# A fourteenth room in a shared arena, paid for with three smaller buffers, and tile 30's output moved from GpSimd to VectorE

## The chip, the cores and the metric

The kernel runs on one core of one Trainium2 chip. The metric is device time in microseconds of one execution, the median over several runs. Engine names in profile rows: PE is the TensorE matmul unit and PEld its weight load, DVE is VectorE, ACT is ScalarE, POOL is GpSimd, and SP is SyncE, which here only issues DMAs. A "q" behind an engine's name means its sequencer, which waits, branches and issues, while the engine itself does not work.

## The reference, cut to what matters

The input x has 8 batches of 512 rows and 512 columns; there are 16 heads of 32 columns. A single token per batch is projected too and added to every query and every key.

```python
Q, K, V = heads(x @ Wq.T + bq), heads(x @ Wk.T + bk), heads(x @ Wv.T + bv)
cQ = Q + heads(cond @ Wq.T + bq)
cK = K + heads(cond @ Wk.T + bk)
attn = softmax(cQ @ cK.T / sqrt(32))        # per batch and head, 512 x 512
out = x + merge_heads(attn @ V)
```

All data are 32-bit floats. The softmax's arguments are shifted by each row's own maximum.

## The kernel before, in words

**Tiles.** The work is cut into T = 32 tiles: tile t is batch t // 4 and head group t % 4, four heads of 32 columns, which fill 128 partitions. A tile needs projections of q, k and v (shared by pairs of tiles), scores with their row maxima (`row_max`, line 617 on PE, lines 584 and 626 on DVE), exponentials on ACT, the product with V on PE (`times_v`, line 745), and at last a division, the bias and the residual x (`send`, lines 811 to 814).

**Two kinds of tiles.** Odd tiles from 1 to 27 are "blocked". `denominators` (line 664) writes their exponentials with queries on the partitions, and the matmul with V needs keys there. So `exchange` sends them through 16 DMAs per half tile, each of which moves 32 partitions of one room to another quarter of the tile `blocks`, and then DVE transposes `blocks` in place in squares of 32 (`turn_blocks`, line 637, eight pieces per tile). All other tiles compute the scores a second time with keys on the partitions; `exponentials` (lines 717 to 734) does this in four steps kc = 0 to 3.

**The arena.** `arena` is a tile of 13 rooms of 4 KB per partition. A blocked tile always uses rooms 0 to 7 (`rows_kept`: rooms 0 to 3 for its first half, 4 to 7 for its second). The other tiles take two rooms per step kc from a counter, which is set to room 8 when the next tile is blocked. Even tile t therefore uses rooms 8, 9 (kc 0), 10, 11 (kc 1), 12 and 0 (kc 2), 1 and 2 (kc 3). The blocked tile t + 1 is being made in the same stretch of time: its first half lies in rooms 0 to 3 and is copied out by `exchange(t + 1, 0)`. Room 0 may be overwritten in step kc 2 only after the four DMAs that read it have landed.

**The order of the work.** For PE, ACT, DVE and POOL the order is that of the source, written out by hand: each tile's turn in the main loop (t = 1 to 28) is four items, "V" (product with V of tile t - 1), "q", "k" and "v" (projections), and each item carries one step of exponentials where t is even, one quarter of the next tile's scores, and small work. DMAs on SP are placed by the framework's planner, which follows the order of the source as far as buffers are free in its own estimate; SP then works through its list in order. DMAs that POOL issues (in `exchange` the sources on partitions 96 to 127, `BY_POOL = (3,)`) stand in POOL's own order.

**Products of blocks.** Projections use seven products of half blocks instead of eight (`MADE_OF`). Four combinations of blocks of x are kept in `xc` (four slots of 2 KB per partition) and made anew for each batch by `combine_x`: lines 385 and 386 for the first half, 388 and 389 for the second, on POOL except for one on DVE. Product 5 uses combination 0, which is x block (0,1) minus x block (0,0). No product uses block (0,1) of x itself.

**Residuals and output.** `load_residual` (line 194) loads x once more for a pair of tiles into one of two buffers with the tag "xr"; `add_bias` (line 207, POOL) adds the bias for v. `send` copies a tile's transposed result to a buffer "res" (two of them) and finishes it on POOL, lines 813 and 814.

**The start.** Tile 0 has its own written order ahead of the loop: four steps of exponentials, each beside one half of a v projection. **The end.** Tiles 29 to 31 have one too. Tile 30's output is finished at lines 1272 to 1275 (DVE transposes, then POOL multiplies by the reciprocal sums and adds the residual), and three of its four stores are issued at line 1280 while tile 31 is finished on DVE and PE (lines 1291 to 1314); the fourth is issued last of all. Line 1352 is the end of the program, where each engine runs a DRAIN and all meet at a barrier.

Of the kernel before, what the change touches and what calls it, by code (L numbers as in the profile page):

```python
# [9 lines left out]
F32 = mybir.dt.float32  # L10
BF16 = mybir.dt.bfloat16
AF = mybir.ActivationFunctionType
ALU = mybir.AluOpType
# [4 lines left out]
def kernel(  # L18
# [38 lines left out]
    nc = tc.nc  # L57
    P = 128
# [4 lines left out]
    HG = P // HD  # L63
# [4 lines left out]
    T = B * G  # L68
    HS = S // 2

    ROOMS = 13
    BY_POOL = (3,)
    WARM = (48, 8, 8)
    BLOCKED = list(range(1, T - 4, 2))
# [1 line left out]
    const = ctx.enter_context(tc.tile_pool(name="const", bufs=1))  # L76
# [5 lines left out]
    op = ctx.enter_context(tc.tile_pool(name="op", bufs=2))  # L82
# [37 lines left out]
    def banks(i, n=1):  # L120

        row = row_of[0] or [at_end[j] for j in TURNS[turn[0]]]
        j = row[i]
        if n == 1:
            return psum[:, j, :]
        k = row[i + 1]
        return psum[:, j : k + 1 : k - j, :]
# [24 lines left out]
    BL = 32  # L152
    NB = S // BL

    def spread(a, d, n=1):

        return a.rearrange("(f j) d -> j f d", j=BL)[:, :, d : d + n * BL]
# [14 lines left out]
    xr = {}  # L172
# [7 lines left out]
    def load_residual(t):  # L180

        b, g = divmod(t, G)
        if t == T - 1:

            xr[t] = xT[b][:, g, :]
        elif late:
            xr[t] = late_part(t % 2 * 10 + 2).rearrange("p (f e) -> p f e", e=BL)
            for h in range(HG):
                nc.sync.dma_start(xr[t][h * BL : (h + 1) * BL], spread(x[b], h * P + g * BL))
        else:  # L190
            two = op.tile([P, NB, 2, BL], F32, tag="xr", name=f"xr_{t}", bufs=2)
            twos[t // 2] = two
            for h in range(HG):
                nc.sync.dma_start(
                    two[h * BL : (h + 1) * BL].rearrange("p f c e -> p f (c e)"),
                    spread(x[b], h * P + g * BL, 2),
                )
            for i in range(2):
                xr[t + i] = two[:, :, i, :]
# [8 lines left out]

    arena = ep.tile([P, ROOMS, NP * S], F32, tag="arena", name="arena")
    place = [0]  # L210

    def room_for_e(t, kc, pr):
# [3 lines left out]
        i = place[0]  # L216
        place[0] = (i + 1) % ROOMS
        return arena[:, i, :].rearrange("p (i s) -> p i s", s=S)
# [102 lines left out]
    condT = early[:, 7, : NC * HD].rearrange("p (c e) -> p c e", e=HD)  # L321
    identb = const.tile([P, P], BF16, tag="identb", name="identb")
    nc.vector.tensor_copy(identb, ident)
    xc = const.tile([P, 4, 2, HS], F32, tag="xc", name="xc")
    vs = [const.tile([P, NS, D], F32, tag=f"v{i}", name=f"v{i}") for i in range(2)]


# [31 lines left out]
    xT = {}  # L359
# [18 lines left out]
    def combine_x(b, half, on=nc.vector):  # L378

        if b >= B:  # L380
            return
        blk = [[xT[b][:, i * 2 : i * 2 + 2, j * HS : (j + 1) * HS] for j in range(2)] for i in range(2)]
        to = [xc[:, i, :, :] for i in range(4)]
        if half == 0:
            on.tensor_tensor(to[2], blk[1][1], blk[0][1], ALU.subtract)
            on.tensor_tensor(to[1], to[2], blk[0][0], ALU.add)
        else:
            on.tensor_tensor(to[0], blk[0][1], blk[0][0], ALU.subtract)
            on.tensor_tensor(to[3], blk[1][0], to[1], ALU.subtract)
# [51 lines left out]

    def block_of_x(b, i, kc, at):
        f = MADE_OF[i - 1][1]
        if isinstance(f, int):
            return xc[:, f, kc, at]
        off = HS * (f == "22")
        return xT[b][:, kc + 2 * (f != "11"), at.start + off : at.stop + off]

    def product(n, b, u, i, pt, kcs=(0, 1)):

        for kc in kcs:
            w = block_of_w(n, i, u, kc)
            if n == "v":
                still, moving = block_of_x(b, i, kc, slice(u * P, (u + 1) * P)), w
            else:
                still, moving = w, block_of_x(b, i, kc, slice(0, HS))
            for j in range(HG):
                r = slice(j * HD, (j + 1) * HD)
                nc.tensor.matmul(  # L459
                    pt[r], still[:, r], moving, start=(kc == kcs[0]), stop=(kc == kcs[-1])  # L460
                )
# [83 lines left out]
    def other_products(n, b, u, dens, small, at):  # L545

        dens()
        one_, two_ = banks(at[0]), banks(at[1])
        product(n, b, u, 4, one_[:, :HS])
        product(n, b, u, 5, one_[:, HS:])  # L550
        small()
        product(n, b, u, 2, two_[:, :HS], (1,))
        product(n, b, u, 3, two_[:, HS:])
        c1, c12, c2, c22 = parts_of(n, b, u)
        nc.vector.tensor_tensor(c12, one_[:, HS:], c12, ALU.add)
        nc.vector.tensor_tensor(c2, halves(one_), twice(c22), ALU.add)
        plus(n, b, u, 0, c1, halves(two_), c1)
        if n != "v":
            for g in range(2):
                qkT[n, b * G + u * 2 + g] = pair_of(b * G + u * 2, n)[:, g, :]  # L560
# [78 lines left out]
    def exchange(t, half):  # L639

        if t not in blocked:
            blocked[t] = room(f"blocks_{t}")
        for g in (0, 2, 1, 3):
            for a in range(HG):
                queue = nc.gpsimd if a in BY_POOL else nc.sync
                of = arena[a * BL : (a + 1) * BL, half * HG + g, :]
                to = blocked[t][g * BL : (g + 1) * BL, a, half * 2 : half * 2 + 2]
                queue.dma_start(to.rearrange("p c h s -> p (c h s)"), of)  # L648

    def denominators(t, qc, w=HG):  # L650

        if t >= T - 2:
            return
        for j in range(HG):
            if t in BLOCKED:
                to = rows_kept(t, qc // 2)[:, :, qc % 2, j, :].rearrange(
                    "p g (c e) -> p g c e", e=BL
                )
            else:
                to = banks(w + j)  # L660
            of = banks(w + j)
            if t in BLOCKED:
                of = of.rearrange("p (c g e) -> p g c e", g=HG, e=BL)
            nc.scalar.activation(  # L664
                to,
                of,
                AF.Exp,
                bias=nmax[t][:, qc, j, :],
                accum_out=sums[t][:, qc, j, :],
            )  # L670
# [137 lines left out]

    def send(t, y_, rec):

        y = op.tile([P, NB, BL], F32, tag="res", name=f"res_{t}", bufs=2)
        nc.vector.transpose(y.rearrange("p f e -> p (f e)"), y_)  # L812
        nc.gpsimd.tensor_tensor(y, y, rec.broadcast_to([P, NB, BL]), ALU.mult)  # L813
        nc.gpsimd.tensor_tensor(xr[t], y, xr[t], ALU.add)  # L814
        if t % 2 or t >= T - 4:
            to_store.append(t)
# [17 lines left out]
    def untranspose(o, pt):  # L834
        for qc in range(NS):
            nc.tensor.transpose(  # L836
                pt[:, qc * P : (qc + 1) * P], o[:, qc * P : (qc + 1) * P], ident
            )
# [136 lines left out]
    def late_part(i):  # L975
        return late[0][:, i, :]
# [36 lines left out]
        )  # L1013
    load_residual(0)
    add_bias(0)
    load_residual(2)

    exponentials(0, 0)
    row_max(1, 1)
# [20 lines left out]
    exponentials(0, 3)  # L1040
    row_max(2, 0)
    other_products("v", 0, 1, lambda: denominators(2, 0), nothing, (0, 2))

    def products(t, n, blocks, hold, dens, small):

# [35 lines left out]
    for t in range(1, T - 3):  # L1081
        b, r = divmod(t, G)
# [116 lines left out]
    t = T - 3  # L1199
# [22 lines left out]
    t = T - 2  # L1222
# [28 lines left out]
    t = T - 1  # L1251
# [17 lines left out]
    rec = op.tile([P, NB, 1], F32, tag="recs", name=f"recs_{t - 1}")  # L1269
    nc.vector.reciprocal(rec, den[:, :, 0:1])  # L1270
    y30 = late_part(13).rearrange("p (f e) -> p f e", e=BL)
    nc.vector.transpose(y30.rearrange("p f e -> p (f e)"), parts[t - 1])
    x30 = xr.pop(t - 1)
    nc.gpsimd.tensor_tensor(y30, y30, rec.broadcast_to([P, NB, BL]), ALU.mult)
    nc.gpsimd.tensor_tensor(y30, y30, x30, ALU.add)

    def store_30(queue, hs):
        b, g = divmod(t - 1, G)
        for h in hs:
            queue.dma_start(spread(out[b], h * P + g * BL), y30[h * BL : (h + 1) * BL])  # L1280

    store_30(nc.sync, (0, 1))
    exponentials(t, 3, (4, 2, 0, 1))
    times_v(t, 2, pv)
    pd = bank(7)
# [5 lines left out]
    nc.vector.tensor_tensor(part_x, pd, xr[t], ALU.mult)  # L1291
    den = late_part(11)
    nc.scalar.copy(den, pd)
    store_30(nc.scalar, (2,))
    oT = late[0][:, 0, :]
    y = late[0][:, 1, :].rearrange("p (c s) -> p c s", c=NS)
    rec = op.tile([P, NS, HG, 1], F32, tag="rec", name="rec")
    pi, po = bank(6), [bank(4), bank(2)]
    b, g = divmod(t, G)
    two = [slice(0, HS), slice(HS, S)]  # L1300
    for i in range(2):
        nc.vector.tensor_tensor(oT[:, two[i]], pv[:, two[i]], part_x[:, two[i]], ALU.add)  # L1302
        for qc in (i * 2, i * 2 + 1):
            nc.tensor.transpose(  # L1304
                po[i][:, qc * P : (qc + 1) * P], oT[:, qc * P : (qc + 1) * P], ident
            )
        if i == 0:
            untranspose(den, pi)
    nc.vector.reciprocal(  # L1309
        rec, pi.rearrange("p (c h e) -> p c h e", c=NS, h=HG)[:, :, :, 0:1]  # L1310
    )
# [45 lines left out]
```

## Time and profile before

| what | value |
|---|---|
| median of 3 runs | 681.99 us (680.9, 681.99, 684.14) |
| profiled execution | 682.65 us, of which the span from first to last instruction is 680.4 us |
| PE busy | 660.6 us, 97% |
| DVE busy | 578.9 us, 85% |
| ACT busy | 544.6 us, 80% |
| POOL busy | 340.7 us, 50% |
| mean granted TensorE clock | 0.994 |

The page's first part gives busy time per engine. The timeline lists instructions in order of time with their start, duration and count; the bracket at a row's end is the engine's idle time just ahead of it and what ended it. The view of a source line lists all instructions that bear its number with shortest, median and longest duration and the start of the first and the last.

### The profile page before, as it was taken

To read this page: it belongs to the slowest core of one execution; us is meant where nothing else is said; L and a number is where in the kernel's file an instruction comes from. 1 tells how busy PE (TensorE), PEld (TensorE's weight loads), DVE (VectorE), ACT (ScalarE), POOL (GpSimd) and SP (SyncE) were. 2 spreads that over 40 slices of the span, in tenths; PEclk is the share of its full clock that TensorE was granted. 3 is DMA by queue.
4 is the path that set the end of the run, shared out by engine and by line. 5 is a ranking of instruction groups with operands and counts; after the bars stand their busy time and mean duration, and the time that the engine had idled before them with its cause. 6 is when DMAs were issued, how large, how long until landed. Compare 5 with 4: busy or idle time off the path is not lost. (4 is left out here: it accounts for less than half of the span.)

```text
span 680.4 us, 22874 instructions
## 1 busy us (share of the span) xinstructions
PE 660.6 (97%) x9100; PEld 312.6 (46%) x9100; DVE 578.9 (85%) x821; ACT 544.6 (80%) x1397; POOL 340.7 (50%) x449
## 2 busy tenths in 40 slices
PE   7989999999999999999999999999999999999993
PEld 6444454544544444444544444454544544454421
DVE  5897988989899898979889897898989898897793
ACT  1568788988979898898889888788988989897771
POOL 5551563565446464466635664464644666352531
PEclk9999999999999999999999999999999999999997
DMA  9718439386574938658383865729376573822011
GB/s 203 129 29 206 126 68 224 69 200 152 128 190 85 223 79 209 142 133 208 71 223 70 211 139 134 188 67 237 80 201 151 132 178 66 220 47 56 16 18 32
DMA packets 140814, 90.85 MB, mean 134 GB/s; under 512 B 117436, under 2 KB 126308, under 8 KB 140708
## 3 DMA queue, kind: packets, MB, share of 16 engines
q1 hardware_dynamic: 132196, 73.78, 47.5%
q0 software_dynamic: 5568, 14.95, 8.7%
q8 instruction: 72, 1.18, 0.8%
q10 hardware_dynamic: 2944, 0.66, 0.5%
q14 instruction: 34, 0.28, 0.1%
HBM read 20.27 MB, written 8.39 MB: 42 GB/s over the span
## 5 line engine op out<-in xcount | busy, mean ns | idle before, releaser
L664 ACT ACTIVATE psum<-psum,nmax 128x512 f32<-128x512 f32 x256 | 169.0, 663 | 52.5 <-DVE nmax L584 40.1
L584 DVE TENSOR_REDUCE nmax<-psum 128x1 f32<-128x512 f32 x270 | 171.4, 680 | 46.0 <-PE psum L617 45.5
L734 ACT ACTIVATE arena<-psum 128x512 f32<-128x512 f32 x264 | 136.9, 602 | 33.8 <-PE psum L723 24.4
L617 PE MATMUL psum<-kT,qT 32*128 32x512 f32 x1024 | 157.5, 621 | 1.4 <-ACT psum L664 1.4
L664 ACT ACTIVATE arena<-psum,nmax 128x512 f32<-128x512 f32 x224 | 152.6, 697 | 5.3 <-issue 4.2
L626 DVE TENSOR_REDUCE nmax<-psum 128x2 f32<-128x1024 f32 x115 | 139.3, 1212 | 1.1 <-PE psum L617 1.1
L637 DVE STREAM_TRANSPOSE blocks<-blocks 128x1024 f32<-128x1024 f32 x112 | 132.2, 1218 | 0.3 <-DMA blocks<-arena 0.2
L648 POOL DMA_DIRECT2D blocks<-arena x112 | 56.1, 506 | 78.8 <-ACT arena L664 69.2
L813 POOL TENSOR_TENSOR res<-res,recs 128x512 f32<-128x512 f32 x30 | 31.5, 1049 | 120.9 <-DVE res L812 120.9
L617 PEld LDWEIGHTS psum<-kT,qT 32*128 32x128 f32 x1024 | 59.5, 182 | 64.9 <-issue 24.0
L745 PE MATMUL psum<-arena,v 128*32 128x512 f32 x576 | 69.4, 597 | 0.0
L723 PE MATMUL psum<-qT,kT 32*128 32x512 f32 x528 | 68.5, 589 | 0.0
L745 PE MATMUL psum<-blocks,v 128*32 128x256 f32 x896 | 52.1, 381 | 0.0
L459 PE MATMUL psum<-wc_v,xc 128*32 128x256 f32 x768 | 50.6, 381 | 1.4 <-ACT v L497 1.4
L664 ACT ACTIVATION_READ_ACCUMULATOR psum<-psum,nmax 128x1 f32 x256 | 51.9, 203 | 0.0
L664 ACT ACTIVATION_READ_ACCUMULATOR arena<-psum,nmax 128x1 f32 x224 | 47.8, 213 | 0.0
L459 PE MATMUL psum<-xc,wc_q 128*32 128x256 f32 x720 | 47.4, 381 | 0.0
L459 PE MATMUL psum<-xc,wc_k 128*32 128x256 f32 x720 | 47.4, 381 | 0.0
L812 DVE STREAM_TRANSPOSE res<-psum 128x512 f32<-128x512 f32 x28 | 20.1, 717 | 23.3 <-PE psum L745 23.3
L814 POOL TENSOR_TENSOR xr<-res,xr 128x512 f32<-128x512 f32 x30 | 38.5, 1282 | 2.4
L207 POOL TENSOR_TENSOR xr<-xr,wT_q 128x512 f32<-128x512 f32 x30 | 38.4, 1279 | 0.2
L745 PEld LDWEIGHTS psum<-blocks,v 128*32 128x32 f32 x896 | 26.4, 110 | 25.0 <-ACT arena L734 10.6
(184 smaller groups left out, 934.4 us busy)
## 6 DMA issues: line engine op xcount, KB each, us to landing
blocks<-arena SPq DMA_DIRECT2D x336, 128.0 KB, 3.8
blocks<-arena POOLq DMA_DIRECT2D x112, 128.0 KB, 3.9
xr<-in_x_dram SPq DMA_DIRECT2D x60, 128.0 KB, 2.6
x<-in_x_dram SPq DMA_DIRECT2D x56, 128.0 KB, 3.5
out_dram<-xr SPq DMA_DIRECT2D x56, 128.0 KB, 2.4
w_q<-in_L_cond_Wq_dram SPq DMA_DIRECT2D x4, 256.0 KB, 4.4
w_k<-in_L_cond_Wk_dram SPq DMA_DIRECT2D x4, 256.0 KB
w_v<-in_L_cond_Wv_dram SPq DMA_DIRECT2D x4, 256.0 KB, 8.3
```

Source lines behind the costliest of these rows:

```text
L207: nc.gpsimd.tensor_tensor(xr[t], xr[t], bias, ALU.add)
L459: nc.tensor.matmul(pt[r], still[:, r], moving, start=(kc == kcs[0]), stop=(kc == kcs[-1]))
L584: nc.vector.tensor_reduce(nmax[t][:, qc, j : j + 1, 0], pt, AX.X, ALU.max, negate=True)
L617: nc.tensor.matmul(pt, qkT["q", t][r, qc * P : (qc + 1) * P], qkT["k", t][r, :], start=True, stop=True,)
L626: nc.vector.tensor_reduce(nmax[t][:, qc, pr * 2 : pr * 2 + 2, 0], pt, AX.X, ALU.max, negate=True)
L637: nc.vector.transpose(e, e)
L648: queue.dma_start(to.rearrange("p c h s -> p (c h s)"), of)
L664: nc.scalar.activation(to, of, AF.Exp, bias=nmax[t][:, qc, j, :], accum_out=sums[t][:, qc, j, :],)
L723: nc.tensor.matmul(bank[j], qkT["k", t][r, kc * P : (kc + 1) * P], qkT["q", t][r, :], start=False, stop=True,)
L734: nc.scalar.activation(e[:, i, :], bank[pr * 2 + i], AF.Exp)
L745: nc.tensor.matmul(pt[j * HD : (j + 1) * HD, at], vs[b % 2][:, kc, (g * HG + j) * HD : (g * HG + j + 1) * HD], e, start=(kc == chunks[0]), ...
L814: nc.gpsimd.tensor_tensor(xr[t], y, xr[t], ALU.add)
```

## The change

- `ROOMS` goes from 13 to 14. An even tile then uses rooms 8 and 9, 10 and 11, 12 and 13, 0 and 1.
- The room is paid for by 4 KB per partition elsewhere: `res` has one buffer instead of two (2 KB), and `xc` three slots instead of four (2 KB). Combination 0 is made in place over block (0,1) of x for batches 1 to 7; for batch 0, whose x is still needed whole, it lies in one of the two "xr" buffers until tile pair 2 takes that buffer.
- `load_residual(2)` moves from ahead of tile 0's four steps to behind them, since its buffer is taken until then.
- `exchange` issues the groups in the order 0, 1, 2, 3 instead of 0, 2, 1, 3.
- Tile 30: the multiplication goes from POOL to DVE at the same place, and the addition goes to DVE behind tile 31's two additions at line 1302 and ahead of the reciprocal at line 1309. The three stores follow the addition.

```diff
-    ROOMS = 13
+    ROOMS = 14
...
-    xc = const.tile([P, 4, 2, HS], F32, tag="xc", name="xc")
+    xc = const.tile([P, 3, 2, HS], F32, tag="xc", name="xc")
+    x0c = op.tile([P, 2, 2, HS], F32, tag="xr", name="x0c", bufs=2)[:, 0]
+
+    def in_place(b):
+
+        return xT[b][:, 0:2, HS:] if b else x0c
...
-        to = [xc[:, i, :, :] for i in range(4)]
+        to = [in_place(b), *(xc[:, i, :, :] for i in range(3))]
...
         f = MADE_OF[i - 1][1]
+        if f == 0:
+            return in_place(b)[:, kc, at]
         if isinstance(f, int):
-            return xc[:, f, kc, at]
+            return xc[:, f - 1, kc, at]
...
-        for g in (0, 2, 1, 3):
+        for g in range(HG):
...
-        y = op.tile([P, NB, BL], F32, tag="res", name=f"res_{t}", bufs=2)
+        y = op.tile([P, NB, BL], F32, tag="res", name=f"res_{t}", bufs=1)
...
     add_bias(0)
-    load_residual(2)
...
     other_products("v", 0, 1, lambda: denominators(2, 0), nothing, (0, 2))
+    load_residual(2)
...
-    nc.gpsimd.tensor_tensor(y30, y30, rec.broadcast_to([P, NB, BL]), ALU.mult)
-    nc.gpsimd.tensor_tensor(y30, y30, x30, ALU.add)
+    nc.vector.tensor_tensor(y30, y30, rec.broadcast_to([P, NB, BL]), ALU.mult)
...
-    store_30(nc.sync, (0, 1))
...
-    store_30(nc.scalar, (2,))
...
         if i == 0:
             untranspose(den, pi)
+    nc.vector.tensor_tensor(y30, y30, x30, ALU.add)
+    store_30(nc.sync, (0, 1))
+    store_30(nc.scalar, (2,))
     nc.vector.reciprocal(
```

## The prediction

> **What bounds the kernel now.** I read the page first, then the table of waits, then the timeline at three places: the start, one turn of the loop, and the end.
>
> ```profile
> span 680.4 us, 22874 instructions
> PE 660.6 (97%) x9100; PEld 312.6 (46%) x9100; DVE 578.9 (85%) x821; ACT 544.6 (80%) x1397; POOL 340.7 (50%) x449
> ```
>
> PE is busy 97% of the span, and no row of the change takes a matmul away. So it can gain only where PE is kept waiting, and behind PE's last work. There are three such places.
>
> *Start.* ACT, PE and SP, timeline (start, duration, both in us):
>
> ```profile
> 59.33 1.09 ACT L734 ACTIVATE arena<-psum 128x512 f32<-128x512 f32 x2
> 62.83 1.09 ACT L734 ACTIVATE arena<-psum 128x512 f32<-128x512 f32 x2 [2.42 <-DMA blocks<-arena]
> ...
> 47.49 0.40 PE L720 MATMUL psum<-wT_v,onesb 3*128 3x512 bf16 x4
> 52.72 0.40 PE L720 MATMUL psum<-wT_v,onesb 3*128 3x512 bf16 x4
> 58.05 0.39 PE L720 MATMUL psum<-wT_v,onesb 3*128 3x512 bf16 x4
> 65.24 0.73 PE L720 MATMUL psum<-wT_v,onesb 3*128 3x512 bf16 x4
> 71.15 1.14 PE L617 MATMUL psum<-kT,qT 32*128 32x512 f32 x8
> ...
> 51.03 2.84 SPq L194 DMA_DIRECT2D xr<-in_x_dram  x4
> 55.56 2.39 SPq L167 DMA_DIRECT2D x<-in_x_dram  x4
> 58.26 17.96 SPq L648 DMA_DIRECT2D blocks<-arena  x24
> 85.42 1.33 SPq L694 DMA_TRANSPOSE wT_v<-split  x1
> ```
>
> In step kc 2 of tile 0 ACT writes room 12 at 59.33, then stands 2.42 us for the DMAs that read room 0, which SP began to issue at 58.26. PE pays: the steps begin at 47.49, 52.72 and 58.05, 5.23 and 5.33 apart. The next is 7.19 later, and the one behind it 5.91. Against 5.23 and 5.33 that is 1.96 + 0.58 = 2.5 us lost.
>
> *Loop.* ACT's first exponentials in the turns of tiles 2, 24 and 26, and step kc 2 and 3 of tile 4:
>
> ```profile
> 91.12 2.06 ACT L734 ACTIVATE arena<-psum 128x512 f32<-128x512 f32 x4
> 528.19 2.06 ACT L734 ACTIVATE arena<-psum 128x512 f32<-128x512 f32 x4
> 567.62 1.57 ACT L734 ACTIVATE arena<-psum 128x512 f32<-128x512 f32 x3
> ...
> 141.53 1.08 ACT L734 ACTIVATE arena<-psum 128x512 f32<-128x512 f32 x2
> 143.78 1.08 ACT L734 ACTIVATE arena<-psum 128x512 f32<-128x512 f32 x2 [1.17 <-issue]
> 147.42 1.59 ACT L734 ACTIVATE arena<-psum 128x512 f32<-128x512 f32 x3
> ```
>
> Two turns without a wait take 567.62 - 528.19 = 39.43 us. The twelve pairs of turns from 91.12 to 567.62 take 476.50, where 12 x 39.43 = 473.16: 3.34 us are lost in some of them. Tile 4 shows how: the first two of step kc 2 (room 12) run at 141.53, the next two (room 0) come 1.17 us late. The view names "issue" as the cause, but POOL's share of the copy tells it:
>
> ```profile
> 138.83 2.00 POOL L648 DMA_DIRECT2D blocks<-arena  x4
> DMA to landing us min/median/max: 2.3/3.8/6.5
> 501.69 2.12 SPq L648 DMA_DIRECT2D blocks<-arena  x2
> 509.18 1.23 DVE L637 STREAM_TRANSPOSE blocks<-blocks 128x1024 f32<-128x1024 f32 x1
> ```
>
> POOL issues the read of room 0's last quarter at 138.83. With 3.8 us to land, the median of these DMAs, it is done at 142.6, the moment at which ACT is ready (141.53 + 1.08). Each landing over the median stalls ACT, and PE behind it. It is a lottery drawn anew in each turn; the runs' spread from 680.9 to 684.14 is of the same size.
>
> *End.* The rows of line 1352, the end of the program, SP's wait there, and the last work of each engine:
>
> ```profile
> L1352 POOLq DRAIN x3: 46/102/11037, 668.6 to 680.1; - x3
> L1352 SPq DRAIN x3: 7/7/7, 674.8 to 679.9; - x3
> L1352 DVEq DRAIN x2: 19/340/661, 670.7 to 679.9; - x2
> SPq L1352 <- PEq L1352: 5.0, 1, 5.0
> 651.96 1.27 POOL L814 TENSOR_TENSOR xr<-res,xr 128x512 f32<-128x512 f32 x1
> 666.76 0.65 DVE L1272 STREAM_TRANSPOSE late<-parts 128x512 f32<-128x512 f32 x1
> 667.97 0.69 DVE L1291 TENSOR_TENSOR late<-psum,xT 128x512 f32<-128x512 f32 x1 [0.55 <-PE psum L755]
> 668.62 1.27 POOL L1275 TENSOR_TENSOR late<-late 128x512 f32<-128x512 f32 x1
> 668.80 0.76 DVE L1302 TENSOR_TENSOR late<-psum,late 128x256 f32<-128x256 f32 x2
> 669.92 0.85 SPq L1280 DMA_DIRECT2D out_dram<-late  x2
> 670.19 0.26 DVE L1309 RECIPROCAL rec<-psum 128x16 f32<-128x16 f32 x1 [0.63 <-PE psum L836]
> ```
>
> The longest of POOL's three drains takes 11.04 us. The first starts at 668.6, the last at 680.1, so only the first can be that long: it ends at 679.6. SP has seen all stores land and drains at 674.8, then waits 5.0 us at the barrier. So the span is ended by POOL's drain, not by the chain of waits through PE and DVE. Its end lies 9.73 us behind POOL's last operation, the addition of tile 30 (668.62 + 1.27 = 669.89).
>
> **The change part by part.**
>
> *Room 14, start.* Step kc 2 of tile 0 goes to rooms 12 and 13; nothing reads 13. The wait of 2.42 us goes. Room 0 is next wanted in step kc 3, which PE begins at 65.24 - 2.5 = 62.7 and whose exponentials follow 1.3 us later, as 59.33 follows 58.05: at 64.0. SP's three DMAs that read it are the first at 58.26, 17.96 / 24 = 0.75 us apart; the third goes out at 59.8 and, with a median landing (3.8 us), is done at 63.6. Room 1 follows by 0.5 to 1 us on both sides. That is tight, but no longer late. Bounds -2.5 (PE's count) to 0; I take -2.4, ACT's own row.
>
> *Room 14, loop.* Room 0 is wanted at step kc 3, 147.42 - 143.78 = 3.64 us later than now, room 1 1.0 us behind it. The plain order lets group 1 go out second, so both have some 4 us of margin where room 0 has none. All 3.34 us go; bounds -3.34 and 0.
>
> *Plain order of groups.* The same 32 DMAs. What waits for all four groups is DVE's first transpose: in the tightest tile SP has issued at 503.81 and DVE comes at 509.18, 5.4 us later, against landings of 3.8, at most 6.5. Cost 0; no row shows neighbouring groups in this order, so its upper end is the slower rival below, its lower end 0.
>
> *One "res".* DVE's copy must now wait until POOL has read the copy before.
>
> ```profile
> L813 POOL TENSOR_TENSOR res<-res,recs 128x512 f32<-128x512 f32 x30 | 31.5, 1049 | 120.9 <-DVE res L812 120.9
> ```
>
> POOL waits for DVE's copy (120.9 us over 30), not the other way round: the buffer is long free. 0.
>
> *Combination in place.* The same POOL operation, 1.28 us. A price would come if waits went by whole stretches of xT, for product 1's operand lies between the two pieces written:
>
> ```profile
> 157.15 1.07 PE L459 MATMUL psum<-xT,wT_q 128*32 128x256 f32 x16
> 159.38 1.29 POOL L388 TENSOR_TENSOR xc<-xT 128x512 f32<-128x512 f32 x1
> ...
> 106.89 8.41 SPq L648 DMA_DIRECT2D blocks<-arena  x12
> 111.54 1.23 DVE L637 STREAM_TRANSPOSE blocks<-blocks 128x1024 f32<-128x1024 f32 x1
> ```
>
> PE would then wait 160.67 - 157.15 = 3.5 us in seven batches, 24.6 us. But DVE's transpose at 111.54, whose pieces lie on both sides of what the second half's DMAs write, runs while those are still being issued (to 115.30). Waits go by exact elements: 0, upper end 24.6.
>
> *Residual 2.* Its four DMAs (2.84 us of SP) leave 51.03 and go behind the step in which PE last reads the buffer, 65.24 to 71.15. SP is not sooner free for the copies: x at 55.56 stands ahead of them. Behind them SP has nothing from 76.22 to 85.42, so 2.84 us fit. If the planner puts them ahead of the copy's second half, that lands 2.1 to 2.8 us later and can meet DVE's transposes: between 0 and +0.5; I take 0.
>
> *Tile 30 on VectorE.* POOL loses two operations, so its last one is the row at 651.96. DVE gains two. A like operation, 128x512 with both inputs in SBUF:
>
> ```profile
> 65.72 0.68 DVE L385 TENSOR_TENSOR xc<-xT 128x512 f32<-128x512 f32 x1
> ```
>
> The multiplication fits at 667.41, where DVE is idle 0.55 us until PE is done: 0.68 - 0.55 = 0.13 late for line 1291, which line 1302 hides (it waits for PE until 668.8). The addition starts at 669.56 and ends at 670.24; DVE was idle 0.63 there, the reciprocal comes 0.05 late. The stores go out at 670.3 instead of 669.92, ahead of tile 31's at 671.0. Cost +0.1, at most +0.7 (one whole operation). And the drain: if it follows POOL's last operation by 9.73 us, it ends near 653.23 + 9.73 = 663, and SP's drain at 674.84 opens the barrier: 679.62 - 674.84 = 4.78 less. Bounds -4.78 and 0; I take -4.7. For it: DVE's drain (670.7 + 0.66) ends when DVE is through with its own last work, so a drain looks at its engine; and no other row of the trace ends near 679.6.
>
> The Trainium skill ("VectorE: DVE Perf Modes", "The DRAIN you can't avoid") says that the drains of a program's start and end take about 12 ns on all five engines; SP's 7 ns agree, POOL's 11.04 us do not, and the row decides. "PSUM — Partial Sum Buffer" ("Engine vs sequencer instructions") says that a drain waits for its own engine to be idle, which is the reading taken.
>
> *Sum*, against the profiled execution: 682.65 - 2.4 - 3.34 - 4.7 + 0.1 = 672.3. That execution stands 0.66 over the median of the runs, by its draw of loop waits, which the change removes; so the sum needs no correction to that median. **Forecast 672.3 us**, 1.4% under 681.99. Half a per cent, 3.4 us, is about what a measurement of this kernel can tell from no change.
>
> **The rivals.**
>
> *The drain does not follow POOL's last operation* but something that stays where it is, such as the last stores. For it: only one drain of this kind is in the trace, so no row shows its dependence. Against: SP sees the last store 5 us earlier. Then 682.65 - 5.7 + 0.1 = 677.0.
>
> *The start keeps its wait*: SP's order or the landing of room 0 at 64.4 takes back the 2.4. Then 674.7. With a lottery that only moves to step kc 3, up to 678.
>
> *Slower: the plain order makes the copies land later.* Place: DVE's first transpose in each of the 14 blocked tiles. With a margin of about 2.5 us over the median landing, a median of 7.6 us (twice 3.8) costs 14 x (3.8 - 2.5) = 18 us: 690. It decides from a landing of about 7.0, where 14 x (3.2 - 2.5) eats the 10.3 gained. For it: nothing but that no row shows this order. Against: landings of 6.5 at most now, with up to three DMAs to one group in a row already.
>
> The Trainium skill ("SBUF — State Buffer", "Door 1: The DMA port swizzle") states that partitions 32 apart share a DMA port and 64 apart do not, which speaks for this rival: groups 0 and 1, now neighbours, write through the same eight ports. By its 27.2 GB/s a port, 128 KB take an estimated 0.6 us on eight ports, about SP's issue time, so later landings by its figures would be tenths of a us, not four; no run so far shows it.
>
> *Slower by waits on whole stretches of xT*: 672.3 + 24.6 = 697.
>
> **How the numbers follow.** Forecast 0.66 (own range 671 to 674.2); drain elsewhere 0.14; start or lottery stays 0.11 (0.03 of it together with the drain rival: 679.4); slower by landings 0.05, by stretches 0.02; 0.02 for a mix near no change. Faster by over 0.5%: 0.66 + 0.14 + 0.08 = 0.88; within 0.05; slower 0.07. The range runs from 671.0 (the forecast less 0.1 for the start by PE's count, 0.1 for no cost at the end, and 1.1 for scatter, a third of the runs' spread of 3.24) to 677.6, so that it takes in the drain rival with the same scatter halved.
>
> **What would show it.** No wait of ACT at line 734 for copies; twelve pairs of turns at 39.43 each; the start's steps 5.3 apart; POOL's drain over by about 658 and SP's drain followed at once by the barrier; DVE's reciprocal within 0.2 us of PE's last transpose. It is wrong if POOL's drain still ends some 5 us behind SP's, or if DVE's line 637 begins to wait for DMAs.

## The result, and the profile after

The changed kernel takes 671.93 us (median of 4 runs, 671.82 to 672.39); on the same chip the kernel before took 682.2 (4 runs, 680.9 to 684.14). The ratio is 0.9851, with a 95% interval from 0.9834 to 0.9867. The forecast was 672.3. The profiled execution took 671.82 us, with this span (page, first part):

```profile
span 669.9 us, 22890 instructions
PE 657.6 (98%) x9100; PEld 312.0 (47%) x9100; DVE 579.6 (87%) x823; ACT 544.0 (81%) x1397; POOL 337.8 (50%) x447
```

The span is 10.5 us shorter than the 680.4 of before, while PE's busy time fell by only 3.0 us: most of what went was time in which PE did no work. Part of those 3.0 us looks like waiting too: in the twelve pairs of turns of the loop (below) the same 6722 matmuls are booked with 475.42 us before and 473.34 after, at a granted clock of 1.00 in both. Line numbers have moved: 734 is now 741, 664 is 671, 648 is 655, 637 is 644, 1352 is 1359.

*Start.* Timeline of ACT, PE and SP, as before (start and duration in us):

```profile
59.05 2.07 ACT L741 ACTIVATE arena<-psum 128x512 f32<-128x512 f32 x4 [0.23 <-PE psum L730]
64.48 2.06 ACT L741 ACTIVATE arena<-psum 128x512 f32<-128x512 f32 x4 [0.30 <-ACT arena L671]
...
47.22 0.40 PE L727 MATMUL psum<-wT_v,onesb 3*128 3x512 bf16 x4
52.44 0.39 PE L727 MATMUL psum<-wT_v,onesb 3*128 3x512 bf16 x4
57.77 0.39 PE L727 MATMUL psum<-wT_v,onesb 3*128 3x512 bf16 x4
63.15 0.40 PE L727 MATMUL psum<-wT_v,onesb 3*128 3x512 bf16 x4
68.46 1.14 PE L624 MATMUL psum<-kT,qT 32*128 32x512 f32 x8
...
53.53 1.28 SPq L655 DMA_DIRECT2D blocks<-arena  x2
55.06 2.49 SPq L167 DMA_DIRECT2D x<-in_x_dram  x4
57.59 16.72 SPq L655 DMA_DIRECT2D blocks<-arena  x22
74.41 2.19 SPq L194 DMA_DIRECT2D xr<-in_x_dram  x4
```

The four exponentials of step kc 2 now run in one piece at 59.05. The steps on PE are 5.22, 5.33, 5.38 and 5.31 apart. From the first to the work behind the fourth it takes 21.24 us, where it took 23.66 before (47.49 to 71.15): 2.42 less. The first step itself begins 0.27 sooner (47.22 against 47.49), ahead of everything that the change touches in ACT and the arena.

*Loop.* ACT's first exponentials of tiles 2, 24 and 26, and then the two rows of the table of waits (total, count, longest, in us) in which ACT waits at line 741 for no named engine, and DVE at line 644 for a copy:

```profile
88.43 1.08 ACT L741 ACTIVATE arena<-psum 128x512 f32<-128x512 f32 x2
522.34 1.09 ACT L741 ACTIVATE arena<-psum 128x512 f32<-128x512 f32 x2
561.77 1.58 ACT L741 ACTIVATE arena<-psum 128x512 f32<-128x512 f32 x3
...
ACT arena L741 <- issue: 1.7, 1, 1.7
DVE blocks L644 <- DMA blocks<-arena: 0.2, 1, 0.2
```

The twelve pairs take 561.77 - 88.43 = 473.34 us, 3.16 less than the 476.50 of before, and within 0.2 of twelve times 39.43. In the table of waits no row is left in which ACT waits for the copies (before: once, 2.4 us).

*Copies.* The rows of the DMA issues (KB each, median us from issue to landing). Before, the medians were 3.8 on SP and 3.9 on POOL:

```profile
blocks<-arena SPq DMA_DIRECT2D x336, 128.0 KB, 4.1
blocks<-arena POOLq DMA_DIRECT2D x112, 128.0 KB, 4.1
```

*End.* The end of the program, SP's wait there, and the last work of POOL and DVE:

```profile
L1359 POOLq DRAIN x3: 46/102/11032, 646.1 to 669.6; - x3
L1359 SPq DRAIN x3: 7/7/13, 669.1 to 669.4; - x3
SPq L1359 <- PEq L1359: 0.7, 2, 0.5
646.12 1.26 POOL L821 TENSOR_TENSOR xr<-res,xr 128x512 f32<-128x512 f32 x1
661.60 0.69 DVE L1281 TENSOR_TENSOR late<-late,recs 128x512 f32<-128x512 f32 x1
662.99 0.76 DVE L1306 TENSOR_TENSOR late<-psum,late 128x256 f32<-128x256 f32 x2
663.67 0.68 DVE L1313 TENSOR_TENSOR late<-late 128x512 f32<-128x512 f32 x1
664.39 0.26 DVE L1316 RECIPROCAL rec<-psum 128x16 f32<-128x16 f32 x1
```

POOL's long drain begins at 646.1 and ends at 657.1, 9.73 us behind its last operation (646.12 + 1.26 = 647.38) and 12 us ahead of SP's. SP drains at 669.15 and the barrier opens at once: 0.5 us at most, where it stood for 5.0. DVE's reciprocal starts 0.03 us behind PE's last transpose (664.36).

Put together, the 10.5 us of span are 0.27 ahead of the first step, 2.42 at the start, 3.16 in the loop and 4.63 behind the last even turn.

### The profile page after: what moved, and what is told of

The parts are those of the page before. It is cut to its first block, busy times and chain, and to the rows that moved or that the text cites. A ratio compares the mean times of both kernels' runs of the same rounds, so it can differ in the third digit from the quotient of the medians.

```text
span 669.9 us, 22890 instructions
## 1 busy us (share of the span) xinstructions
PE 657.6 (98%) x9100; PEld 312.0 (47%) x9100; DVE 579.6 (87%) x823; ACT 544.0 (81%) x1397; POOL 337.8 (50%) x447
## 5 line engine op out<-in xcount | busy, mean ns | idle before, releaser
L624 PE MATMUL psum<-kT,qT 32*128 32x512 f32 x1024 | 155.6, 621 | 1.4 <-ACT psum L671 1.4
L466 PE MATMUL psum<-wT_v,xT 128*32 128x256 f32 x512 | 34.2, 382 | 0.0
L466 PE MATMUL psum<-wc_v,xc 128*32 128x256 f32 x512 | 33.5, 379 | 0.0
L533 POOL TENSOR_TENSOR v<-v 128x512 f32<-128x512 f32 x14 | 17.9, 1275 | 29.7 <-ACT v L527 29.7
```

Source lines behind the costliest of these rows:

```text
L466: nc.tensor.matmul(pt[r], still[:, r], moving, start=(kc == kcs[0]), stop=(kc == kcs[-1]))
L624: nc.tensor.matmul(pt, qkT["q", t][r, qc * P : (qc + 1) * P], qkT["k", t][r, :], start=True, stop=True,)
```

## The experiments

All ratios are to the kernel before on the same chip, with 95% intervals. In three sets of runs it took 683.01, 683.37 and 683.39 us.

| run | time, us | ratio |
|---|---|---|
| tail alone | 676.86 (675.53 to 680.82) | 0.9924 [0.9891, 0.9957] |
| rooms alone | 678.05 (676.72 to 678.82) | 0.991 [0.9878, 0.9942] |
| both, the changed kernel again | 672.54 (671.94 to 673.93) | 0.9837 [0.9802, 0.9872] |
| 13 rooms, all else changed | 678.45 (677.65 to 680.84) | 0.9943 [0.9922, 0.9964] |
| old order of groups | 672.43 (672.39 to 674.33) | 0.9865 [0.9844, 0.9886] |
| a small copy on POOL | 675.84 (675.76 to 675.84) | 0.9892 [0.9871, 0.9913] |
| the same, later | 677.58 (677.49 to 677.66) | 0.9918 [0.9891, 0.9945] |
| a store issued by POOL | 678.57 (678.55 to 679.88) | 0.9937 [0.9918, 0.9957] |
| last store early | 673.44 (672.12 to 673.72) | 0.987 [0.985, 0.9889] |
| last store early, again | 673.58 (672.15 to 674.41) | 0.9845 [0.9814, 0.9877] |

### Two halves of the change, each alone

The first run is the kernel before with only tile 30's output on VectorE:

```diff
-    nc.gpsimd.tensor_tensor(y30, y30, rec.broadcast_to([P, NB, BL]), ALU.mult)
-    nc.gpsimd.tensor_tensor(y30, y30, x30, ALU.add)
+    nc.vector.tensor_tensor(y30, y30, rec.broadcast_to([P, NB, BL]), ALU.mult)
...
-    store_30(nc.sync, (0, 1))
...
-    store_30(nc.scalar, (2,))
...
+    nc.vector.tensor_tensor(y30, y30, x30, ALU.add)
+    store_30(nc.sync, (0, 1))
+    store_30(nc.scalar, (2,))
```

> The kernel before with tile 30's multiplication and addition on VectorE and its stores behind them; nothing else changed. My theory (POOL's drain ends some 9.7 us behind POOL's last operation, and that alone set the end): 4.7 less than before, about 677.5 us; POOL's long drain is over by about 664, SP's last drain opens the barrier; ACT's wait of 2.4 us in tile 0 and the scattered waits in the loop stay, and so does the scatter of the runs. Rival (the end is set by something else, and the shorter end of the changed kernel comes of the other parts): 682 us, POOL's drain still some 5 us behind SP's.

Its ratio of 0.9924 is 5.2 us of 683; the median of 676.86 is 0.6 under the forecast. Its runs lie apart: four at 675.53 to 676.86 with a mean granted clock of 0.997 to 0.999, three at 679.88 to 680.82 with 0.991 to 0.993. The rows of POOL's last operation and of the end:

```profile
649.79 1.27 POOL L814 TENSOR_TENSOR xr<-res,xr 128x512 f32<-128x512 f32 x1
L1352 POOLq DRAIN x3: 46/102/11033, 649.8 to 673.3; - x3
L1352 SPq DRAIN x3: 7/7/13, 672.8 to 673.1; - x3
```

POOL's drain is over at 660.8, and SP's at 672.8 ends the program. The start still shows ACT's wait: the fourth step begins at 65.26, 7.23 behind the third at 58.03. The loop keeps waits, but smaller ones: the twelve pairs of turns take 474.30 us (91.14 to 565.44), 1.0 over the changed kernel's 473.34, where the kernel before was 3.2 over it.

The second is the changed kernel with that half taken back, so that the arena's part stands alone:

```diff
-    nc.vector.tensor_tensor(y30, y30, rec.broadcast_to([P, NB, BL]), ALU.mult)
+    nc.gpsimd.tensor_tensor(y30, y30, rec.broadcast_to([P, NB, BL]), ALU.mult)
+    nc.gpsimd.tensor_tensor(y30, y30, x30, ALU.add)
...
+    store_30(nc.sync, (0, 1))
...
+    store_30(nc.scalar, (2,))
...
-    nc.vector.tensor_tensor(y30, y30, x30, ALU.add)
-    store_30(nc.sync, (0, 1))
-    store_30(nc.scalar, (2,))
```

> The changed kernel with tile 30's output back on POOL, as in the kernel before. If the gains of the end and of the arena are independent, this kernel has the start and the loop of the changed kernel (steps of the start 5.2 to 5.4 us apart, twelve pairs of turns in 473.3 us) and the end of the kernel before (POOL's drain ends 9.73 us behind its last operation, some 4.8 us behind SP's): 671.93 + 4.79 - 0.16 = 676.6 us. If the output on VectorE only removed something that the loop's changes would have hidden as well, it stays below 674.

The median of 678.05 lies 1.4 above the forecast, the fastest run (676.72) on it. The profiled execution took 678.66; it has all the parts that were named: steps of the start 5.23, 5.33, 5.40 and 5.31 apart, pairs of turns in 473.38 us, and SP standing 5.0 us at the barrier:

```profile
664.88 1.27 POOL L1282 TENSOR_TENSOR late<-late 128x512 f32<-128x512 f32 x1
L1359 POOLq DRAIN x3: 46/102/11038, 664.8 to 676.4; - x3
L1359 SPq DRAIN x3: 7/7/13, 671.0 to 676.1; - x3
SPq L1359 <- PEq L1359: 5.5, 2, 5.0
```

It is late from the start on: its first step begins at 49.24 instead of 47.22. Why shows in a table by stretches of time (length, busy time of PE, PEld, DVE, ACT and POOL with their counts of instructions, then the granted TensorE clock, the DMAs' share and GB/s):

```profile
12.00:16.00 4.00, 4.00 (x18) 3.25 (x17) 1.54 (x4) 0.00 (x0) 3.70 (x3) 0.58 1.24 223
```

PE worked at 0.58 of its clock from 12 to 16 us, and did 18 matmuls there. The changed kernel's profile has 86 in the same stretch, at 1.00:

```profile
12.00:16.00 4.00, 4.00 (x86) 3.28 (x85) 1.85 (x6) 0.00 (x0) 3.92 (x4) 1.00 1.24 224
```

That is a disturbance of the start which the edit, at the end of the kernel, cannot reach, and it comes back below. Of the six runs, the three with a clock of 0.993 took 678.64 to 678.82 us, the three with 0.994 and 0.995 took 676.72 to 677.46. The two ratios multiply to 0.9924 x 0.991 = 0.9835, and the changed kernel itself, on the same chip as the second, gives this:

> The changed kernel itself, as the measure for the two beside it: 671.9 us, ratio to the kernel before 0.985.

Measured was 0.9837. So the two halves add up, as far as these intervals reach, which is some 3 us. The profile of rooms alone says it more sharply: its start, its loop and its barrier are each as the changed kernel and the kernel before have them.

### 13 rooms

The changed kernel with one room taken away and everything else kept:

```diff
-    ROOMS = 14
+    ROOMS = 13
```

> The changed kernel with 13 rooms; its plain order, its later residual 2, its one output copy and its combination in place stay. My theory (the fourteenth room alone removes the waits): room 0 is wanted in step kc 2 again. In tile 0 ACT waits 1.5 to 2.4 us (SP's first two copies now leave at 53.5, the third at 57.6, which lands at 60 to 62, and ACT is ready at 60); in the loop 0 to 1.5 us in some turns, 1 to 5 us together: 674.5 to 678 us. Rival (residual 2's move frees SP, and the plain order does the rest; the room is not needed): 671.9 to 672.5 us with no wait over 0.3 us at the exponentials.

678.45 is half a us over the upper end. The wait at the start is back, larger than before and, at 3.13 us, than the 1.5 to 2.4 expected, which is enough for that half us. ACT's exponentials of step kc 2, and SP's issues:

```profile
61.43 1.09 ACT L741 ACTIVATE arena<-psum 128x512 f32<-128x512 f32 x2 [0.38 <-PE psum L730]
65.64 1.09 ACT L741 ACTIVATE arena<-psum 128x512 f32<-128x512 f32 x2 [3.13 <-DMA blocks<-arena]
...
55.91 1.29 SPq L655 DMA_DIRECT2D blocks<-arena  x2
57.43 2.40 SPq L167 DMA_DIRECT2D x<-in_x_dram  x4
59.87 6.15 SPq L655 DMA_DIRECT2D blocks<-arena  x8
```

Two copies go out ahead of the loads of x, the third behind them, at 59.87. The room is free only when that one has landed. The loop's pairs take 475.89 us, 2.7 over the undisturbed 473.16, with single late exponentials as in the kernel before (1.56 us in the turn of tile 4). So it is the room that removes both losses; the new order of groups and the later residual do not do it without the room. The profiled execution took 680.84, 2.4 over the median, and there the clock falls twice:

```profile
40.00:44.00 4.00, 3.82 (x40) 2.03 (x44) 2.56 (x4) 1.99 (x8) 2.65 (x8) 0.57 0.02 4
...
68.00:72.00 4.00, 4.00 (x36) 1.57 (x32) 1.88 (x4) 2.93 (x9) 2.02 (x5) 0.62 0.39 97
```

Each fall is to half of the clock for 3.41 us and costs an estimated 1.7 us where PE is the bound (half of 3.41). The second begins at 67.6, just behind the stretch in which PE stood 2.47 us because of ACT's wait.

### The old order of groups

```diff
-        for g in range(HG):
+        for g in (0, 2, 1, 3):
```

> The changed kernel with the groups in the old order 0, 2, 1, 3. My theory (room 1 is wanted 1 us behind room 0 in step kc 3, with some 3 to 4 us of margin in the loop): 671.9 us, within 0.5; in tile 0 the copies that read room 1 leave 2 us later and ACT may wait up to 1 us there. Second question, the landing: 4.1 us in the changed kernel, 3.8 before. If the plain order makes neighbouring groups share ports, the median goes back to 3.8 here; if the 0.3 us come of something else it stays at 4.1.

672.43, no difference from the changed kernel that these runs can show. In tile 0 ACT did not wait for room 1 either: it stood 0.27 us ahead of step kc 3, for its own work. The landings go back to what they were:

```profile
blocks<-arena SPq DMA_DIRECT2D x336, 128.0 KB, 3.8
blocks<-arena POOLq DMA_DIRECT2D x112, 128.0 KB, 3.8
```

In all kernels with the plain order SP's median is 4.0 to 4.1, in those with the old order (this one, the tail alone, the kernel before) 3.8; POOL's is 3.9 to 4.1 against 3.7 to 3.9. So the plain order does make the copies land later, by 0.2 to 0.3 us on SP, and the pairs of turns take as long with the one as with the other (473.67 and 473.34).

### What POOL's drain follows

The kernels before and after leave open whether the drain follows POOL's last work, and from its start or its end. So a copy of one column (128x1) was put on POOL behind tile 30's reciprocal; it writes to a place that nothing reads, and the computation is otherwise the whole one:

```diff
     nc.vector.reciprocal(rec, den[:, :, 0:1])
+    nc.gpsimd.tensor_copy(late_part(14)[:, :1], rec[:, 0, :])
```

> The changed kernel with one more POOL operation, a copy of 128x1 numbers (the first of tile 30's reciprocals) to an unused place, which can run at about 661.1 in a span that ends at 669.9. Theory A (the drain ends 9.7 us behind the end of POOL's last operation, however small): the drain ends at 661.3 + 9.7 = 671.0, 1.9 behind SP's drain at 669.15: 673.8 us. Theory B (the drain takes 11.03 us from its own start, which comes when the last operation starts): 672.1, 674.8 us. Theory C (its length goes with the work that POOL still has to finish, so a small copy costs little): 671.9 us.

```profile
663.26 0.19 POOL L1278 COPY late<-recs 128x1 f32<-128x1 f32 x1 [13.68 <-DVE recs L1277]
L1360 POOLq DRAIN x3: 46/102/9938, 663.2 to 673.7; - x3
L1360 SPq DRAIN x3: 7/7/13, 671.3 to 673.4; - x3
```

The drain starts at 663.24 and takes 9.94 us; it ends at 673.18, 9.73 us behind the copy's end (663.45), as behind the addition of 1.27 us. A drain of 11.03 us from its own start would have ended at 674.3. So a copy of 0.19 us holds the drain as long as an operation of 1.27. By the time alone theory B (674.8) would be nearer than A (673.8); the drain's own start and end decide. The time of 675.84 is 2.0 over the forecast: this execution's first exponentials start 1.96 us later than the changed kernel's (50.46 against 48.50), with the clock at 0.59 from 40 to 44 us.

The same copy behind tile 31's reciprocal, the last moment at which POOL could be given work:

```diff
         rec, pi.rearrange("p (c h e) -> p c h e", c=NS, h=HG)[:, :, :, 0:1]
     )
+    nc.gpsimd.tensor_copy(late_part(14)[:, :1], rec[:, 0, 0, :])
```

> The same with the copy 3.7 us later, behind tile 31's reciprocal (over at 664.6). Theory A: the drain ends at 664.9 + 9.7 = 674.6, 5.5 behind SP's: 677.3 us, 3.6 over the kernel with the earlier copy. Theory B: 678.4 us, also 3.6 over it. Theory C: 671.9 us.

```profile
664.94 0.19 POOL L1319 COPY late<-rec 128x1 f32<-128x1 f32 x1 [17.33 <-DVE rec L1316]
L1360 POOLq DRAIN x3: 46/102/9940, 664.9 to 675.4; - x3
```

664.92 + 9.94 = 674.86, again 9.73 behind the copy's end. The copy started 1.68 us later than the first, and the drain ended 1.68 later. The time of 677.58 is 0.3 over theory A (677.3) and 0.8 under theory B (678.4). It is 1.7 and not 3.6 over the kernel with the earlier copy, since that one ran 2.0 late.

And no computation on POOL at all, but the issue of tile 30's third store:

```diff
-    store_30(nc.scalar, (2,))
+    store_30(nc.gpsimd, (2,))
```

> The changed kernel with tile 30's third store issued by POOL instead of ACT, at about 664.4 to 664.9; POOL gets no other operation. If the drain follows any work of POOL, the issue of a DMA too: it ends at 664.9 + 9.7 = 674.6, 677.3 us. If only operations on data count: the drain has nothing new to wait for behind the issue, SP's drain still opens the barrier, and the time is 671.9 us within 0.4.

```profile
666.71 0.72 POOL L1286 DMA_DIRECT2D out_dram<-late  x1 [17.27 <-DVE rec L1316]
L1359 POOLq DRAIN x3: 46/102/10531, 666.7 to 677.7; - x3
```

666.68 + 10.53 = 677.22, 9.79 behind the end of the issue. Even one DMA issue counts. The median is 1.3 over the forecast. This profile too has the clock at 0.57 from 12 to 16 us, and PE's last transposes begin at 666.25, where the changed kernel's began at 664.19; with that 2.06 taken off, the issue still ends 0.5 later than the 664.9 of the forecast.

### The last store

The fourth store of tile 30 was issued last of all; here it goes out with the third:

```diff
-    store_30(nc.scalar, (2,))
+    store_30(nc.scalar, (2, 3))
...
-    store_30(nc.scalar, (3,))
```

> The changed kernel with tile 30's fourth store issued by ACT right behind the third instead of last of all. My theory (with POOL's drain out of the way the landing of the last store sets the end, and ACT stands from 664.8 to 665.2 anyway): the last issue ends at about 666.8 instead of 667.2, 0.3 to 0.4 us less, 671.5 us. Rival (the DMA engines are full at the end and the last byte lands when it did): 671.9 us. Rival (tile 31's first store on ACT is pushed back): 672.2 us.

> The last store of tile 30 issued together with the third instead of last of all, measured beside the changed kernel. If the last store's issue on ACT's queue sets the end, 0.4 us less than the changed kernel; if SP's drain waits for tile 31's stores instead, the same within 0.2 us, as the stretch behind the last even turn (107.33 against 107.38 us) says.

Not shown to be better. Beside the changed kernel on the same chip it took 673.58 against 672.54, with overlapping runs. In the profiles, the stretch from the last even turn's first exponential to SP's drain is 107.33 us in both of its executions, and 107.38 in both of the changed kernel's. The first expectation, that it gains 0.4, is wrong: the issue of the last store does not set the end. That the landing of tile 31's stores does is the reading that is left; no run isolates it. The higher times beside the changed kernel go with lower clocks (0.994 to 0.997 against 0.997 to 0.999).

## Why the prediction was right

**Start: -2.4, measured -2.42.** ACT's wait went as a whole, and step kc 3 did not inherit it. The bracket at 64.48 is 0.30 us and names ACT's own work. That was the tight place of the working (room 0 free at 63.6, wanted at 64.0). The 13-room run shows that the room did it.

One sentence in the working failed. It said that SP is not sooner free for the copies when residual 2 moves, since x stands ahead of them. The planner used the gap: two copies go out at 53.53 *ahead* of x, the other 22 from 57.59 (before: all 24 from 58.26), and residual 2 goes behind all of them at 74.41. With 14 rooms the third copy that reads room 0 so left at 57.59, where the working had 59.8; whether ACT would have waited without that, no run isolates. With 13 rooms it was no help, since the third copy that reads room 0 stayed behind x and left at 59.87.

**Loop: -3.34, measured -3.16.** The turns are at their length without waits, all pairs between 39.41 and 39.55. Of the rest of 0.18, 0.12 lie in the first pair, which takes 39.54 or 39.55 with 13 rooms and with 14. How much the loop loses differs from execution to execution, 3.2 us here, 1.0 and 2.6 over 473.34 in the profiles of tail alone and 13 rooms. The forecast does not hang on that, since it takes off the losses of the execution that it starts from; what the change is worth against another execution does.

The lottery was half right. It is not drawn in each turn: in all three profiles with 13 rooms the late pairs of turns are those that begin with tiles 4, 14 and 18 (before 40.68, 39.64 and 41.05 us, tail alone 39.74, 39.60 and 39.83, 13 rooms 41.08, 39.77 and 40.01), and no other but the first is more than 0.1 over 39.43. The size is what is drawn. Why these three turns, no run shows.

A second reading beside it was wrong in part: that the spread of the runs of before is this lottery. The mean granted clock of each run tells more. Of the 28 runs of the kernel before in the three sets, four of the five slowest (686.04 to 688.28 us) had clocks of 0.987 or 0.988, and the six at 0.995 averaged 681.55 us. A straight line through all 28 gives 0.56 us for each 0.001 of clock, and takes the standard deviation from 1.9 to 1.2 us. So more than half of the variance goes with the clock, and only what is left can be the landings. The changed kernel kept a spread of 2 us in its second set (671.94 to 673.93), with no such landings to wait for: its two slowest runs had a clock of 0.997 (as had one of 672.42), the fastest 0.999.

**End: -4.7, measured -4.79 at the barrier; tile 30: +0.1, measured +0.16.** From the last even turn's first exponential to SP's drain it takes 107.38 us instead of 107.22, and SP's drain is now the end. The drain follows POOL's last work at 9.73 us, as assumed, and where the addition stays on POOL (rooms alone) the 5.0 us at the barrier stay too. The rival in which the drain is tied to the stores (677.0) falls with the small copy: its drain ended at 673.18, 9.73 behind the copy, though the stores had not moved. The addition on DVE found the gap that the working named and cost 0.03 us ahead of the reciprocal. "VectorE: DVE Perf Modes" of the Trainium skill, "The DRAIN you can't avoid", gives about 12 ns for such drains on all engines; every kernel here shows 9.9 to 11.0 us for the longest of POOL's. The reading taken from the Trainium skill's page "PSUM — Partial Sum Buffer", "Engine vs sequencer instructions", that a drain waits for its own engine to be idle, held.

**What was costed at nothing.** Plain order: the landings rose by 0.2 to 0.3 us and nothing waits for them. DVE at line 644 waits for a copy once, for 0.2 us, as before. "SBUF — State Buffer" of the Trainium skill, "Door 1: The DMA port swizzle", has groups 32 partitions apart on the same ports; the order that puts them side by side is indeed the slower, by tenths of a us, which is what the prediction had estimated from that page. That the ports are the cause, no run shows. The slower rival (690) needed landings of 7. Combination in place: product 1 does not wait for it, or the pairs of turns would be longer; the rival of 697 is gone. One "res": nothing.

The sum was 0.37 over the median. Two gains were no term of it. The 0.27 us ahead of the first step lie where executions of one kernel differ by more than that (first step at 47.22 and 47.87 in two profiles of the changed kernel). And 0.33 us lie outside the span: 682.65 - 680.4 = 2.25 before, 671.82 - 669.9 = 1.92 after; what they are, the profiles do not show. The upper end of the prediction's own range, 674.2, is given without its working.

## What to carry to other kernels

Look at which engine's drain ends last: in every kernel here POOL's ends 9.7 to 9.8 us behind its last work, so the last 10 us of such a program should have nothing on POOL, not even a DMA issue, and an operation that is cheap there (1.27 us) can cost 5. A buffer that is reused at the median landing of a DMA stalls by an amount that changes from execution to execution; one room more removes the waits, and their size in one execution can be read beforehand as the difference between the sum of the turns and the turn without a wait. Before a spread between runs of one kernel is put down to a cause in the kernel, set it against the mean granted clock of the same runs. Between kernels that mean misleads, since it takes in the stretch behind PE's last work: before, the clock is at half from 671.9 to the end of the span, and these 8.5 us alone make its mean 0.994.

## What the runs showed of the hardware that was not expected

**POOL's drain has a fixed tail.** It ends 9.73 us behind the last computation, be that 0.19 or 1.27 us long, and 9.79 behind a DMA issue. The drains of DVE, ACT and PE's loader last 0.66, 0.15 and 0.81 us in the same place.

**The clock falls for 3.41 us early in some executions**, to half, at a place that is not the same each time: from about 12 us (rooms alone, the store on POOL), from 39 to 40 (13 rooms, the small copy, the last store early again), or from 67.6 (13 rooms). Ahead of the places near 12 and 40 PE works with gaps: its longest is 1.1 to 2.3 us near 9, and 1.4 with 0.6 behind it near 37. The changed kernel has these gaps as well, and its clock did not fall there in either profiled execution. In every execution the clock also falls behind PE's last work.

The traces show what decides it. Within one execution the falls begin a whole number of steps of 3.413 us apart: with 13 rooms at 40.33, at 67.63 and, behind PE's last work, at 675.21, which is 8 and 186 steps behind the first. In the four other profiles with an early fall, 185 or 193 whole steps lie between it and the last one. PE in the step ahead of each of the first two falls and in the fall (length, PE busy with its count of matmuls, granted clock, the DMAs' share and GB/s):

```profile
36.92:40.33 3.41, 1.44 (x16) 1.00 0.00 0
40.33:43.74 3.41, 3.41 (x36) 0.50 0.02 5
...
64.22:67.63 3.41, 0.94 (x20) 1.00 0.92 207
67.63:71.04 3.41, 3.41 (x28) 0.50 0.34 77
```

Cut each of the twelve profiles into its own steps, counted back from the fall behind PE's last work: the clock was halved behind every step in which PE stood for 1.89 us or more of the 3.41, and behind no other, the idlest of which has 1.79. So it is not the length of one gap that counts but how much idle time of PE falls into one step, and where the steps lie is another matter in each execution. "TensorE: Matmul & The Clock Gate" of the Trainium skill, Part 1, has a free-running window of about 3.4 us, after an idle one of which the clock is halved. Its length and the free running agree with these traces; a window that is idle as a whole was not needed, 1.89 us of it were enough.

That also bears on the kernel before and its wait at the start. There the idlest step around the wait had 1.38 us, and 1.55 in tail alone, and no fall came of it; with 13 rooms the longer wait put 2.47 us into one step, and the fall at 67.63 followed. Whether the runs of before that were not profiled had falls from that place, no trace shows.
